# Row sums of attention weights: pairs of key chunks added by accumulating DMA, with bias rows and the adjacency's cast moved to DMA

## The chip, the cores and the metric

One core of one Trainium2 chip. The time is device microseconds of one execution; each kernel was run several times and medians are quoted. Engine names in the profile: PE is TensorE's matmuls, PEld its weight loads, DVE is VectorE, ACT is ScalarE, POOL is GpSimd, SP is SyncE.

## The reference, cut to what matters

Two attention layers over 32 graphs of 512 nodes and 256 channels, 8 heads. Layer 0 has an MLP; layer 1 has none. The mask of layer 0 is the adjacency or its transpose or the diagonal; that of layer 1 is the adjacency.

```python
scores = jnp.einsum('bhqd,bhkd->bhqk', q * scale, k)
scores = jnp.where(allowed[:, None], scores, -jnp.inf)
attn = jax.nn.softmax(scores, axis=-1)
ctx = jnp.einsum('bhqk,bhkd->bhqd', attn, v)
# ... Wo, bias, residual, layernorm, MLP, residual, layernorm; a second layer alike, without the MLP
```

All biases in the inputs are zero, so a wrong or missing bias would not be seen in the result.

## The kernel before

The work runs in 64 slots, one per graph and layer. In a slot the weights are made in eight steps, one for each of two head groups times four chunks of 128 keys: scores on PE, exp on ACT, mask product on DVE, then two products on PE. One gives the context (psA), the other the row sums by a block of ones (psR).

```python
            def scores(self, layer, k):          # PE, then exp on ACT; one PSUM buffer for s
                ...
                nc.scalar.activation(p, s, AF.Exp, scale=SCALE)     # p: 128 x 2048 f32, bufs=4
            def masked(self, layer, k):          # DVE
                nc.vector.tensor_tensor(p, p, m[:, k % NQ, None, :].to_broadcast([P, HPC, N]), ALU.mult)
            def product(self, layer, k):         # PE
                for j in range(HPC): nc.tensor.matmul(a[...], self.v[...], p[:, j, :], ...)
                for j in range(HPC): nc.tensor.matmul(s[...], ones, p[:, j, :], ...)
                if kc < NQ - 1: return
                # copy of a (ACT); transpose of s, reciprocal, transpose, product with cT (DVE)
```

Between these steps PE gets other work. A **forward** slot carries the output projection and the MLP of the graph that was last in layer 0; an **output** slot finishes the graph that was last in layer 1 and makes the masks, the queries, keys and values of the next one. Masks are made by PE transposes of the adjacency in bf16, and DVE empties both PSUM tiles. The adjacency is loaded as int32 and clamped to bf16 on POOL; bias rows are added to residuals on POOL.

## Time and profile before

| | before |
|---|---|
| time | 3852 us |
| PE busy | 3609 us, 94% |
| forward slot, mean | 70.3 us |
| output slot, mean | 48.7 us |
| mean granted clock | 0.992 |

The slot lengths come from the PE timeline of the profiled execution: from the first scores of one slot to the first scores of the next. Unless two slots are named, they are means over 32 forward and 31 output slots (the last output slot runs into the end of the program). Forward slots are all 70.3 us here; the output slots after the first are 48.3 to 49.3 us. Together these 63 make 3758 us; the rest is the start and the last slot. The prediction shows the lines of four slots. In a line of a group the first number after the bar is the busy time and the second the mean length of one instruction; a figure in square brackets at the end of a timeline line is how long the engine stood idle before it and which engine's work ended that.

### The profile page before, as it was taken

The page shows a single profiled execution, that of the slowest core. Times are in us where ns is not written, and L with a number is a line of the kernel's source. Part 1 is how long each engine was busy: PE and PEld are TensorE (multiplying, and loading weights), DVE is VectorE, ACT ScalarE, POOL GpSimd, SP SyncE. Part 2 cuts the span into 40 slices and gives each one's busy share as a digit, 9 for nine tenths or more (in the row PEclk, how much of TensorE's full clock was granted, in tenths as well). Part 3 has the DMA queues.
Part 4 walks back from the last instruction along what each step waited for, and adds up shares of the span by engine and source line. Part 5 has one row for each costly group of instructions (what it writes and reads, how often), then busy time and mean ns, then how long its engine had stood idle before and what let it go on. Part 6 is the DMA issues. An engine that isn't in the chain of part 4 may idle for free.

```text
span 3851.9 us, 51652 instructions
## 1 busy us (share of the span) xinstructions
PE 3608.8 (94%) x21514; PEld 1885.4 (49%) x21514; DVE 2502.6 (65%) x3461; ACT 1603.0 (42%) x1729; POOL 1376.5 (36%) x1545
## 2 busy tenths in 40 slices
PE   6999999999999999999999999998999999999998
PEld 3544536455364554635546355453554535545354
DVE  3666675766757667576665756667576675666766
ACT  3434444434444344343443444434444344343443
POOL 1333333433334243342433424333242333424332
PEclk9999999999999999999999999999999999999999
DMA  2000000000000000000000000000000100000000
GB/s 86 17 23 13 27 12 17 23 23 17 12 17 23 22 23 6 17 28 17 23 6 17 28 17 23 6 22 23 17 23 6 33 12 17 23 6 34 12 1 12
DMA packets 57553, 75.61 MB, mean 20 GB/s; under 512 B 4448, under 2 KB 40416, under 8 KB 57312
## 3 DMA queue, kind: packets, MB, share of 16 engines
q1 hardware_dynamic: 51776, 67.90, 5.2%
q10 hardware_dynamic: 5536, 4.33, 0.4%
q8 instruction: 170, 2.79, 0.3%
q14 instruction: 71, 0.58, 0.0%
HBM read 55.45 MB, written 16.78 MB: 19 GB/s over the span
## 4 chain that ended last, share of the span: by engine, by line
PE 69%; DVE 23%; POOL 5%; ACT 2%; issue 1%; DMA 0%; ACTq 0%; DVEq 0%; POOLq 0%
PE psQK L260 12%; PE psF L391 12%; PE psH L373 12%; DVE p L282 9%; PE psS L273 8%; PE psA L295 7%; PE psV L245 6%; PE psR L303 6%; PE psO L352 5%; POOL rs L330 4%; DVE st L328 3%; DVE x L411 2%; DVE m L214 2%; ACT p L277 2%; DVE y L341 2%; PE psT L233 1%
## 5 line engine op out<-in xcount | busy, mean ns | idle before, releaser
L277 ACT ACTIVATE p<-psS 128x2048 f32<-128x2048 f32 x512 | 961.9, 1879 | 1167.1 <-PE psS L273 1167.1
L282 DVE TENSOR_TENSOR p<-p,m 128x2048 f32<-128x2048 f32 x512 | 1197.4, 2344 | 273.4 <-ACT p L277 273.4
L330 POOL TENSOR_SCALAR rs<-mv 128x1 f32<-128x1 f32 x512 | 499.2, 975 | 1115.0 <-DVE mv L329 1100.3
L295 PE MATMUL psA<-p,v 128*32 128x512 f32 x4096 | 555.8, 615 | 53.6 <-DVE p L282 53.6
L273 PE MATMUL psS<-qT,kT 32*128 32x512 f32 x4096 | 583.9, 640 | 7.1 <-ACT p L277 2.0
L303 PE MATMUL psR<-p,ones 128*32 128x512 f32 x4096 | 544.6, 604 | 0.0
L314 DVE STREAM_TRANSPOSE sT<-psR 128x512 f32<-128x512 f32 x128 | 91.3, 713 | 643.8 <-PE psR L303 643.8
L391 PE MATMUL psF<-w_L_gnn_W,hT 128*128 128x256 f32 x2048 | 459.1, 382 | 0.0
L373 PE MATMUL psH<-xT,w_L_gnn_W 128*128 128x256 f32 x2048 | 459.1, 382 | 0.0
L391 PEld LDWEIGHTS psF<-w_L_gnn_W,hT 128*128 128x128 f32 x2048 | 383.8, 190 | 100.7 <-ACT cT L311 26.8
L373 PEld LDWEIGHTS psH<-xT,w_L_gnn_W 128*128 128x128 f32 x2048 | 383.8, 190 | 98.2 <-ACT xT L236 24.3
L317 POOL TENSOR_TENSOR total<-total,sT 128x16 f32<-128x16 f32 x128 | 29.0, 227 | 985.6 <-DVE sT L314 985.6
L331 POOL TENSOR_TENSOR rs<-rs,neg_half 128x1 f32<-128x1 f32 x512 | 327.1, 639 | 42.7
L273 PEld LDWEIGHTS psS<-qT,kT 32*128 32x128 f32 x4096 | 159.9, 182 | 332.4 <-issue 187.0
L303 PEld LDWEIGHTS psR<-p,ones 128*32 128x32 f32 x4096 | 135.3, 112 | 314.7 <-issue 305.4
L381 ACT ACTIVATE hT<-psH,c_L_gnn_b 128x256 f32<-128x256 f32 x512 | 215.1, 471 | 171.3 <-PE psH L373 169.2
L260 PE MATMUL psQK<-xT,w_L_gnn_Wqkv 128*128 128x512 f32 x512 | 245.0, 611 | 0.0
L252 ACT COPY v<-psV 128x512 f32<-128x512 f32 x128 | 75.0, 586 | 403.3 <-PE psV L245 403.3
L352 PE MATMUL psO<-w_L_gnn_Wo,cT 128*128 128x256 f32 x1024 | 238.4, 386 | 0.5 <-DVE held L768 0.5
L352 PEld LDWEIGHTS psO<-w_L_gnn_Wo,cT 128*128 128x128 f32 x1024 | 189.2, 190 | 72.3 <-ACT kT L263 47.8
L341 DVE TENSOR_TENSOR y<-psO,x 128x256 f32<-128x256 f32 x256 | 104.1, 407 | 152.5 <-PE psO L352 152.5
L295 PEld LDWEIGHTS psA<-p,v 128*32 128x32 f32 x4096 | 80.9, 108 | 230.1 <-issue 101.9
(64 smaller groups left out, 3476.9 us busy)
## 6 DMA issues: line engine op xcount, KB each, us to landing
adj<-in_adj_dram SPq DMA_DIRECT2D x32, 1024.0 KB, 6.2
x<-in_x_dram SPq DMA_DIRECT2D x32, 512.0 KB, 3.9
out_dram<-x SPq DMA_DIRECT2D x32, 512.0 KB, 2.9
w_L_gnn_W<-in_L_gnn_W_dram ACTq DMA_DIRECT2D x2, 1024.0 KB, 10.8
w_L_gnn_Wqkv<-in_L_gnn_Wqkv_dram SPq DMA_DIRECT2D x1, 768.0 KB, 5.0
w_L_gnn_Wo<-in_L_gnn_Wo_dram ACTq DMA_DIRECT2D x2, 256.0 KB, 5.5
s_L_gnn_bo<-in_L_gnn_bo_dram ACTq DMA_DIRECT2D x2, 128.0 KB, 5.7
s_L_gnn_ln_g<-in_L_gnn_ln_g_dram ACTq DMA_DIRECT2D x2, 128.0 KB, 8.4
```

Of the source, the lines that this page charges most:

```text
L245: nc.tensor.matmul(ps[:, j, :], self.xT[:, i, at], proj[layer][0][2][:, i, :], start=(i == 0), stop=(i == ND - 1),)
L260: nc.tensor.matmul(ps, w[:, i, c * P : (c + 1) * P], self.xT[:, i, :], start=(i == 0), stop=(i == ND - 1))
L273: nc.tensor.matmul(s[:, j, :], self.kT[at, hg, kc * P : (kc + 1) * P], self.qT[at, hg, :], start=True, stop=True)
L277: nc.scalar.activation(p, s, AF.Exp, scale=SCALE)
L282: nc.vector.tensor_tensor(p, p, m[:, k % NQ, None, :].to_broadcast([P, HPC, N]), ALU.mult)
L295: nc.tensor.matmul(a[j * HD : (j + 1) * HD, :], self.v[:, kc, h * HD : (h + 1) * HD], p[:, j, :], start=(kc == 0), stop=(kc == NQ - 1),)
L303: nc.tensor.matmul(s[j * HD : (j + 1) * HD, :], ones, p[:, j, :], start=(kc == 0), stop=(kc == NQ - 1))
L330: nc.gpsimd.tensor_scalar(rs, mv[:, 1:2], EPS, None, ALU.add)
L331: nc.gpsimd.tensor_tensor(rs, rs, neg_half[:, 0:1], ALU.pow)
L352: nc.tensor.matmul(ps[:, j, :], self.cT[:, k, at], wo[layer][:, k, :], start=(k == 0), stop=(k == ND - 1))
L373: nc.tensor.matmul(ps[:, j, :], w1[:, c, at], self.xT[:, c, h * 2 * P : (h + 1) * 2 * P], start=(c == 0), stop=(c == ND - 1),)
L391: nc.tensor.matmul(ps, self.hT[h][:, f, j * P : (j + 1) * P], w2[:, f, :], start=(f == 0), stop=(f == NF - 1))
```

## The change

It takes three of the eight row sums of a slot off PE: an accumulating DMA adds the weights of chunk k+1 to those of chunk k, and PE sums the result once. Only the last pair (6, 7) is left to PE. The accumulating DMAs are issued from POOL, and POOL is relieved of other work: bias rows are added by accumulating DMA too (so x1, onto which one is added, is loaded as well), and the load casts the adjacency. DVE makes two codes from it, edge and none (1 where there is no edge). The mask of layer 1 comes from none and is emptied by ACT in place of DVE. The operations at the ends of slots are put in another order, and some buffers are cut to make room for six p.

```diff
-            nc.gpsimd.tensor_tensor(dst, src, row[:, None, :].to_broadcast([P, NQ, D]), ALU.add)
+            nc.gpsimd.dma_start(out=dst, in_=row[:, None, :].to_broadcast([P, NQ, D]), accum_op=ALU.add)
...
-                nc.vector.tensor_scalar(self.m1[:, i, :], ps, 0.0, None, ALU.not_equal)
+                nc.scalar.activation(self.m1[:, i, :], ps, AF.Copy, bias=1.0, scale=-1.0)
...
-                p = work.tile([P, HPC, N], F32, tag="p", name=f"p_{self.b}_{k}", bufs=4)
+                p = work.tile([P, HPC, N], F32, tag="p", name=f"p_{self.b}_{k}", bufs=6)
...
+            def pair(self, k):
+                nc.gpsimd.dma_start(out=self.p[k], in_=self.p[k + 1], accum_op=ALU.add)
+            def sums(self, k, first=False, last=False):      # the matmuls with ones; if last, DVE's chain
... forward slot:
+            g.pair(0)            # step 3
+            g.pair(2)            # step 5, then g.sums(0, first=True)
+            g.sums(2, last=True) # step 6
+            g.pair(4)            # after product 5; then sums 6, 7 and 4 at the end
... output slot:
+            g.pair(0)            # step 2
                 new.residual()   # step 3: two bias rows, now DMAs
+            g.pair(2)            # step 4
+            g.sums(0, first=True)  # step 5
+            g.sums(2, last=True)   # step 6
+            g.pair(4)            # step 7; then sums 6, 7 and 4
```

More of the change, by code (lines that the diff above doesn't have):

```diff
@@ L166, in value_bias, with add_row @@
                 nc.vector.tensor_tensor(bov[layer], ps, bo[layer], ALU.add)
-        def add_row(dst, src, row):
-            nc.gpsimd.tensor_tensor(dst, src, row[:, None, :].to_broadcast([P, NQ, D]), ALU.add)
+        def add_row(dst, row):
+            nc.gpsimd.dma_start(out=dst, in_=row[:, None, :].to_broadcast([P, NQ, D]), accum_op=ALU.add)
         class Graph:
@@ L183, in load @@
             def load(self):
-                nc.sync.dma_start(
-                    out=self.tile("x", [NQ, D]), in_=x[self.b].rearrange("(c p) d -> p c d", p=P)
-                )
-                nc.sync.dma_start(
-                    out=self.tile("adj", [NQ, N], I32, bufs=1), in_=adj[self.b].rearrange("(c p) k -> p c k", p=P)
+                rows = x[self.b].rearrange("(c p) d -> p c d", p=P)
+                nc.sync.dma_start(out=self.tile("x", [NQ, D]), in_=rows)
+                nc.sync.dma_start(out=self.tile("x1", [NQ, D]), in_=rows)
+                nc.gpsimd.dma_start(
+                    out=self.tile("adj", [NQ, N], BF16, bufs=1), in_=adj[self.b].rearrange("(c p) k -> p c k", p=P)
                 )
             def code(self):
-                code = self.tile("edge", [NQ, N], BF16, bufs=1)
-                for i in range(NQ):
-                    nc.gpsimd.tensor_scalar(code[:, i, :], self.adj[:, i, :], 1.0, -0.25, ALU.min, ALU.max)
+                nc.vector.tensor_scalar(self.tile("edge", [NQ, N], BF16, bufs=1), self.adj, 0.0, None, ALU.max)
+                nc.vector.tensor_scalar(self.tile("none", [NQ, N], BF16, bufs=1), self.adj, 0.0, None, ALU.is_equal)
                 self.tile("m0", [NQ, N], BF16)
@@ L199, in residual @@
             def residual(self):
-                add_row(self.tile("x1", [NQ, D]), self.x, bov[0])
-                add_row(self.x, self.x, be2)
+                add_row(self.x1, bov[0])
+                add_row(self.x, be2)
             def mask0(self, i):
@@ L220, in mask1 @@
                     nc.tensor.matmul(
-                        ps[:, k * P : (k + 1) * P], self.edge[:, k, here], ident_b, start=True, stop=True
+                        ps[:, k * P : (k + 1) * P], self.none[:, k, here], ident_b, start=True, stop=True
                     )
-                nc.vector.tensor_scalar(self.m1[:, i, :], ps, 0.0, None, ALU.not_equal)
+                nc.scalar.activation(self.m1[:, i, :], ps, AF.Copy, bias=1.0, scale=-1.0)
             def transpose(self, src, h):
                 if h == 0:
-                    self.tile("xT", [ND, N])
+                    self.tile("xT", [ND, N], bufs=1)
                 ps = ps_d.tile([P, ND, 2 * P], F32, tag="d", name=f"psT_{self.b}_{h}")
@@ L282, in masked, with product @@
                 nc.vector.tensor_tensor(p, p, m[:, k % NQ, None, :].to_broadcast([P, HPC, N]), ALU.mult)
-            def product(self, layer, k):
+            def product(self, k):
                 hg, kc = divmod(k, NQ)
-                p = self.p.pop(k)
                 if kc == 0:
-                    self.acc[hg] = (
-                        ps_a.tile([P, N], F32, tag="acc", name=f"psA_{self.b}_{hg}"),
-                        ps_a.tile([P, N], F32, tag="sum", name=f"psR_{self.b}_{hg}"),
-                    )
-                a, s = self.acc[hg]
+                    self.acc[hg] = ps_a.tile([P, N], F32, tag="acc", name=f"psA_{self.b}_{hg}")
                 for j in range(HPC):
@@ L295, in product @@
                     nc.tensor.matmul(
-                        a[j * HD : (j + 1) * HD, :],
+                        self.acc[hg][j * HD : (j + 1) * HD, :],
                         self.v[:, kc, h * HD : (h + 1) * HD],
-                        p[:, j, :],
+                        self.p[k][:, j, :],
                         start=(kc == 0),
@@ L301, in product @@
                     )
+                if kc == NQ - 1:
+                    if hg == 0:
+                        self.tile("cT", [ND, N], bufs=1)
+                    nc.scalar.copy(self.cT[:, hg, :], self.acc[hg])
+            def pair(self, k):
+                nc.gpsimd.dma_start(out=self.p[k], in_=self.p[k + 1], accum_op=ALU.add)
+            def sums(self, k, first=False, last=False):
+                hg = k // NQ
+                if first:
+                    self.total = ps_a.tile([P, N], F32, tag="sum", name=f"psR_{self.b}_{hg}")
                 for j in range(HPC):
                     nc.tensor.matmul(
-                        s[j * HD : (j + 1) * HD, :], ones, p[:, j, :], start=(kc == 0), stop=(kc == NQ - 1)
+                        self.total[j * HD : (j + 1) * HD, :], ones, self.p[k][:, j, :], start=first, stop=last
                     )
-                if kc < NQ - 1:
+                if not last:
                     return
-                if hg == 0:
-                    self.tile("cT", [ND, N], bufs=1)
-                cT = self.cT[:, hg, :]
-                nc.scalar.copy(cT, a)
-                sT = small.tile([P, N // HD, HD], F32, tag="sT", name=f"sT_{self.b}_{hg}", bufs=2)
-                nc.vector.transpose(sT.rearrange("p a b -> p (a b)"), s)
+                sT = small.tile([P, N // HD, HD], F32, tag="sT", name=f"sT_{self.b}_{hg}", bufs=1)
+                nc.vector.transpose(sT.rearrange("p a b -> p (a b)"), self.total)
                 r = small.tile([P, N // HD], F32, tag="r", name=f"r_{self.b}_{hg}")
@@ L318, in product @@
                 nc.gpsimd.tensor_tensor(total, total, r, ALU.add)
-                rT = small.tile([P, N], F32, tag="rT", name=f"rT_{self.b}_{hg}", bufs=2)
+                rT = small.tile([P, N], F32, tag="rT", name=f"rT_{self.b}_{hg}", bufs=1)
                 nc.vector.transpose(rT, r[:, :, None].to_broadcast([P, N // HD, HD]))
-                nc.vector.tensor_tensor(cT, cT, rT, ALU.mult)
+                nc.vector.tensor_tensor(self.cT[:, hg, :], self.cT[:, hg, :], rT, ALU.mult)
             def statistics(self, y, n, i):
@@ L383, in residual1 @@
             def residual1(self):
-                add_row(self.x1, self.x1, b2)
+                add_row(self.x1, b2)
                 self.tile("x2", [NQ, D])
@@ L397, in norm2 @@
                 y, stats = self.y.pop(i)
-                z = small.tile([P, D], F32, tag="z", name=f"z_{self.b}_{i}", bufs=3)
+                z = small.tile([P, D], F32, tag="z", name=f"z_{self.b}_{i}", bufs=2)
                 self.affine(z, y, stats, g2, self.x[:, i, :], 2, i)
@@ L442, in slot_forward @@
             if layer == 1:
-                add_row(g.x2, g.x2, bov[1])
+                add_row(g.x2, bov[1])
             last.project(0, 0)
@@ L449, in slot_forward @@
             attend(g, layer, 2)
-            g.product(layer, 0)
+            g.product(0)
             last.norm1(0)
@@ L456, in slot_forward @@
             attend(g, layer, 3)
-            g.product(layer, 1)
+            g.product(1)
+            g.pair(0)
             last.norm1(2)
@@ L466, in slot_forward @@
             last.residual1()
-            if later is not None:
-                later.code()
-            g.product(layer, 2)
+            g.product(2)
             attend(g, layer, 5)
+            g.pair(2)
             for f in range(0, NF, 2):
                 last.hidden(1, f)
-            g.product(layer, 3)
+            g.sums(0, first=True)
+            g.product(3)
             last.mlp(0)
@@ L485, in slot_forward @@
             last.norm3(1)
-            g.product(layer, 4)
+            g.sums(2, last=True)
+            g.product(4)
             g.scores(layer, 7)
@@ L493, in slot_forward @@
             g.masked(layer, 7)
-            g.product(layer, 5)
             last.transpose(last.x2, 0)
-            g.product(layer, 6)
+            g.product(5)
+            g.pair(4)
             last.value(1, 0)
+            g.product(6)
             last.transpose(last.x2, 1)
-            g.product(layer, 7)
+            g.sums(6, first=True)
             last.query_key(1, 0, 0)
             last.query_key(1, 1, 0)
+            g.product(7)
+            g.sums(7)
+            g.sums(4, last=True)
             last.value(1, 1)
+            if later is not None:
+                later.code()
         def slot_output(g, layer, last, new, later):
@@ L512, in slot_output @@
             if layer == 1:
-                add_row(g.x2, g.x2, bov[1])
+                add_row(g.x2, bov[1])
             if last:
@@ L527, in slot_output @@
                 new.transpose(new.x, 0)
-            g.product(layer, 0)
+            g.product(0)
+            g.pair(0)
             attend(g, layer, 3)
@@ L537, in slot_output @@
                 new.residual()
-            g.product(layer, 1)
-            for i in range(NQ):
-                attend(g, layer, 4 + i)
-                if new:
-                    new.mask0(i)
-                    new.mask1(i)
-                g.product(layer, 2 + i)
-            if later is not None:
-                later.code()
+            g.product(1)
+            attend(g, layer, 4)
+            if new:
+                new.mask0(0)
+                new.mask1(0)
+            g.product(2)
+            g.pair(2)
+            attend(g, layer, 5)
+            if new:
+                new.mask0(1)
+                new.mask1(1)
+            g.sums(0, first=True)
+            g.product(3)
+            attend(g, layer, 6)
+            if new:
+                new.mask0(2)
+                new.mask1(2)
+            g.product(4)
+            g.sums(2, last=True)
+            attend(g, layer, 7)
+            if new:
+                new.mask0(3)
+                new.mask1(3)
+            g.product(5)
+            g.pair(4)
             g.masked(layer, 7)
@@ L550, in slot_output @@
                 new.value(0, 0)
-            g.product(layer, 6)
+            g.product(6)
+            g.sums(6, first=True)
             if new:
                 new.query_key(0, 0, 0)
-            g.product(layer, 7)
+                new.query_key(0, 1, 0)
+            g.product(7)
+            g.sums(7)
+            g.sums(4, last=True)
             if new:
-                new.query_key(0, 1, 0)
                 new.value(0, 1)
+            if later is not None:
+                later.code()
         with tc.manual_schedule():
```

## The prediction

> **What bounds the kernel now.** I read the page first: busy time, then the costliest groups.
>
> ```profile
> PE 3608.8 (94%) x21514; PEld 1885.4 (49%) x21514; DVE 2502.6 (65%) x3461; ACT 1603.0 (42%) x1729; POOL 1376.5 (36%) x1545
> ...
> L282 DVE TENSOR_TENSOR p<-p,m 128x2048 f32<-128x2048 f32 x512 | 1197.4, 2344 | 273.4 <-ACT p L277 273.4
> ...
> L303 PE MATMUL psR<-p,ones 128*32 128x512 f32 x4096 | 544.6, 604 | 0.0
> ```
>
> TensorE (PE) is busy 94% of 3852 us. The row sums psR are 4096 instructions, 8 for each of 512 key chunks. 94% is an average, so I cut the timeline into its repeating slots (64: one graph and layer each). There are two kinds. A **forward** slot carries the MLP of the previous graph; an **output** slot carries the masks of the next one. The windows over two output slots and then two forward slots:
>
> ```profile
> core 0: us, PE busy (x) PEld busy (x) DVE busy (x) ACT busy (x) POOL busy (x), PEclk, DMA share, GB/s
> 944.50:992.80 48.30, 43.78 (x284) 18.20 (x281) 35.76 (x40) 20.49 (x17) 20.70 (x18) 0.96 0.04 12
> 992.80:1041.13 48.33, 43.24 (x290) 18.13 (x289) 35.40 (x40) 21.08 (x18) 14.78 (x14) 1.00 0.04 12
> 1041.13:1111.45 70.32, 68.56 (x385) 40.45 (x384) 42.74 (x68) 28.99 (x36) 24.45 (x30) 1.00 0.07 23
> 1111.45:1181.77 70.32, 68.57 (x386) 40.46 (x385) 42.73 (x68) 28.99 (x36) 26.79 (x34) 1.00 0.07 23
> ```
>
> The forward slot is PE-bound (68.6 of 70.3). The output slot has 5 us in which PE waits. 32 x (48.3 + 70.3) = 3796, the rest is start and end. The PE timeline around two early score steps of a forward slot shows a second limit:
>
> ```profile
> 1050.55 1.14 PE L273 MATMUL psS<-qT,kT 32*128 32x512 f32 x8
> 1051.62 1.06 PE L295 MATMUL psA<-p,v 128*32 128x512 f32 x8
> 1052.50 1.04 PE L303 MATMUL psR<-p,ones 128*32 128x512 f32 x8
> 1053.69 1.14 PE L273 MATMUL psS<-qT,kT 32*128 32x512 f32 x8
> ```
>
> By the ACT timeline the exponential of the first psS runs 1051.76 to 1053.64 (1.88 us). There is one psS buffer, so the next scores wait for it: **a score step cannot be shorter than 3.14 us** (1053.69 - 1050.55), whatever PE saves inside it. In the output slot the mask steps follow DVE:
>
> ```profile
> 1024.66 1.88 ACT L277 ACTIVATE p<-psS 128x2048 f32<-128x2048 f32 x1 [2.49 <-PE psS L273]
> ```
> ```profile
> 1026.54 0.38 PE L208 MATMUL psM<-edge,ident_b 128*128 128x512 bf16 x1 [1.95 <-DVE m L214]
> ```
> ```profile
> 1008.15 2.16 POOL L330 TENSOR_SCALAR rs<-mv 128x1 f32<-128x1 f32 x1
> 1010.39 0.58 POOL L331 TENSOR_TENSOR rs<-rs,neg_half 128x1 f32<-128x1 f32 x1
> ```
>
> PE waits 1.95 us for a mask buffer that DVE has not emptied, after the exp had long started; and Pool finishes the fourth rs of the slot only at 1010.97, which is 18.2 us into the slot that began at 992.80.
>
> **What the Trainium skill says.** (1) "DMA: Bandwidth & Descriptors", section SWDGE vs HWDGE vs iDMA: accumulating and casting DMAs can be issued from GpSimd alone, and one SWDGE queue is allocated. The trace of before has no such DMA, so neither is shown. Its section Specifications gives about 1 us to the first byte on that path. (2) "Collectives: The Full Stack", section on the bandwidth ceiling: a reducing DMA is not slowed by the add but by two reads per write, about 31 GB/s per engine halved. Not shown in before either: its plain loads run at 67.9 MB / (5.2% x 3852 us) = 339 GB/s. (3) "SBUF — State Buffer", section Who interferes with whom: a DVE instruction with two SBUF inputs contends with a GpSimd instruction that reads SBUF. The trace agrees: rs takes 0.22 us alone and 2.16 us beside the 2.3 us mask product.
>
> **The change, part by part.** I walk both slots; times are from the slot's start.
>
> *Removed on PE.* Three of eight row sums per slot: 192 groups. A sum that no wait follows costs 0.97 us from its start to the next instruction (by the same timeline 1066.70 to 1067.67), so 192 x 0.97 = 186 us if all counted. They do not.
>
> *Forward slot.* The sums leave steps 2, 3 and 4; the later steps get a sum back for each they lose (0 at step 5, 2 at step 6; 6, 7 and 4 at the end). Step 2 is already 3.14 us: nothing saved. Step 3 was 3.51 and falls to 3.14: 0.4. Step 4 holds 7 us of hidden layer: 0.9 saved. At the end a 1.6 us wait for p goes behind the value product, but that now waits some 1.3 us for its transposed input behind an exp: 0.3. Sum 1.6 us; 32 x 1.6 = **50 us saved**, if the third DMA lands: it is issued after the fourth rs3 (about 58.3) and wanted by sum 4 at about 66, so it has 7.6 us.
>
> *Cost of one accumulate.* 1.05 MB at 16 x 31 / 2 = 248 GB/s is 4.2 us of all engines (estimate from Collectives; doubling the trace's plain 3.1 us gives 6.2). Before it 1.0 us for the descriptors; after it a tail of 1.35 us (the 512 KB store lands in 2.9 us, of which 1.55 is data at 339 GB/s). Issue to landing: 6.5 us. A bias row (512 KB) holds the engines for half as long, 2.1 us.
>
> *Output slot, gains.* Removing Pool's adds (2.4 and 4.5 us, beside which DVE ops took 2.46 for 0.41 and 3.24 for 2.28) and moving m1 to ACT (4 x 0.6) takes some 5.4 us off DVE. With no late DMA I walk PE to 45.7 instead of 48.3.
>
> *Output slot, the new wait.* Pair 0 stands on Pool behind the fourth rs: issued at 18.2, landed at 24.7. PE wants sum 0 at 22.3: **2.4 us late**. Pool then issues the two bias rows, and only then pair 2. On one queue: engines start at 19.2, then 4.2 + 2.1 + 2.1 + 4.2 = 31.8, landed at 33.1. PE, after sum 0 at 25.7, product, scores, masks and product, wants sum 2 at 29.3: **3.8 us late**. DVE's sum chain stands in program order ahead of mask product 6 and of the mask that frees the value's PSUM buffer. So the wait passes through: sums end 34.1, DVE chain 36.7, mask product 39.0, mask 39.6, value 41.6, then product, sum, query/key, product, two sums, value: 51.8. Pair 4 is issued near 36 and lands near 42.5, wanted at 49: in time. The slot is 51.8 - 48.3 = 3.5 longer; 32 x 3.5 = **110 us lost**.
>
> *Start.* The second graph's code now stands on DVE and waits for its cast load before the first mask product: about 4 us, once. ACT gains 128 copies of 0.59 us (75 us) at 42% busy, DVE 64 short operations at slot ends: hidden.
>
> Sum: 3852 - 50 + 110 + 4 = 3916.
>
> **The rivals.** *(a) The accumulate is as fast as a copy* (3.1 us of engines): pair 0 lands at 23.7, pair 2 at 29.9, the output slot is 48.6, about even; 3852 - 50 + 9 + 4 = 3815. For it: the add is free by the skill. Against: two reads. If in addition the landing took under 4 us, the output slot would be 45.7 and the kernel 3720; the store's 2.9 us for half the bytes speaks against that. *(b) Engines at twice the plain time* (6.2 us): pair 2 lands at 39, output slot 57.9, forward slot saves only 0.6: about 4140. Smaller packets or slow descriptor generation (512 rows of 1 KB in each bias row) would look the same. *(c) PE work alone decides* and the DMAs are hidden: 3852 - 186 = 3666. For it: PE is 94% busy. Against: the 3.14 us score step and 18.2 us at which Pool becomes free. *(d) DVE slows down under Pool's descriptor writing*: a few us, since DVE has slack in forward slots.
>
> **Range and chances.** The walk gives 3916, rival (a) 3815, rival (b) 4140. The one number that the profile cannot give is the accumulate's rate. Somebody chose three pairs out of four, which looks like tuning by measurement, so I lean a little to the fast side: 3900. Range 3745 to 4110, wide towards slow since each us of engine time costs the output slot about three. Faster than 3775 needs an accumulate at least as quick as a copy with a short landing: 0.21. Within 2% (3775 to 3929): 0.42. Slower: 0.37.
>
> **What would show it.** Right: psR with 2560 instructions in place of 4096; in output slots PE waits for DMA at psR for p_0 and more for p_2; forward slots near 68.7 us with no DMA wait; output slots near 52; score steps 2 and 3 of the forward slot at 3.14. An accumulate's issue to landing near 6.5 us, pair 2 longer through the queue. Wrong: landings under 4.5 us (then rival a or c), landings over 9 us with waits in forward slots at sum 4 too (b), or a slot that starts pair 0 well before 18 us.

## The result, and the profile after

| | before | after |
|---|---|---|
| time, median | 3851.9 us | 4204.4 us |
| PE busy | 3609 us | 3599 us |
| forward slot, mean | 70.3 us | 71.8 us |
| output slot, mean | 48.7 us | 57.7 us |
| mean granted clock | 0.992 | 0.952 |

The ratio is 1.091 (95% interval 1.089 to 1.093). The time lies above the whole stated range.

The page of the changed kernel, with busy times, the group that sums rows, and the DMA issues from POOL (count, size, median us from issue to landing):

```profile
PE 3598.5 (86%) x19978; PEld 1839.2 (44%) x19978; DVE 2318.3 (55%) x3397; ACT 1664.3 (40%) x1857; POOL 1248.4 (30%) x1641
...
L311 PE MATMUL psR<-p,ones 128*32 128x512 f32 x2560 | 380.8, 687 | 297.1 <-DMA p<-p 297.0
...
p<-p POOLq DMA_DIRECT2D x192, 1024.0 KB, 8.1
...
x<-bov POOLq DMA_DIRECT2D x64, 512.0 KB, 9.0
...
x<-s_L_gnn_ln_b POOLq DMA_DIRECT2D x32, 512.0 KB, 13.8
x<-s_L_gnn_b POOLq DMA_DIRECT2D x32, 512.0 KB, 5.5
```

PE lost 1536 instructions of psR and 164 us of its busy time, and 297 us of waiting for the pairs' DMA stand in front of what is left. The total busy time of PE fell by only 10 us, although fewer instructions run. The windows over two output and two forward slots that follow each other tell where:

```profile
core 0: us, PE busy (x) PEld busy (x) DVE busy (x) ACT busy (x) POOL busy (x), PEclk, DMA share, GB/s
1017.54:1076.39 58.85, 44.09 (x265) 17.43 (x264) 31.36 (x38) 23.09 (x22) 15.44 (x19) 0.91 0.56 99
1076.39:1135.18 58.79, 45.17 (x265) 17.61 (x265) 31.40 (x39) 23.10 (x22) 13.21 (x17) 0.91 0.43 81
1135.18:1206.25 71.07, 66.88 (x361) 39.46 (x360) 41.03 (x69) 28.86 (x36) 23.83 (x33) 1.00 0.32 67
1206.25:1277.33 71.08, 66.89 (x362) 39.47 (x361) 41.01 (x68) 28.85 (x36) 25.71 (x34) 1.00 0.42 82
```

These two output slots are among the longest (the others after the first last 57.0 to 59.1 us), and these two forward slots among the shortest. Over all slots the output slot grew by 9.1 us and the forward slot by 1.5: 32 x 10.6 = 339 us of the 341 between the two profiled spans (3851.9 and 4193.2). The granted clock in the two output slots is 0.91. The timeline of PE in the second output slot shows both waits and the slow instructions behind them:

```profile
1102.72 1.93 PE L311 MATMUL psR<-p,ones 128*32 128x512 f32 x8 [3.94 <-DMA p<-p]
1104.43 1.94 PE L289 MATMUL psA<-p,v 128*32 128x512 f32 x8
1106.29 2.09 PE L272 MATMUL psS<-qT,kT 32*128 32x512 f32 x8
...
1115.45 1.88 PE L311 MATMUL psR<-p,ones 128*32 128x512 f32 x8 [5.05 <-DMA p<-p]
1117.26 1.97 PE L272 MATMUL psS<-qT,kT 32*128 32x512 f32 x8
```

PE waits 3.94 us for pair 0, and from 26.3 us in the slot the three groups of the same kinds that took 1.04, 1.06 and 1.14 us before take about 2. It then waits 5.05 us for pair 2, which it can use at 39.06 us. The timeline of POOL in the same slot, and SP's single DMA in it:

```profile
1094.56 0.91 POOL L303 DMA_DIRECT2D p<-p  x1
1095.57 1.30 POOL L169 DMA_DIRECT2D x<-bov  x1
1096.34 1.83 POOL L169 DMA_DIRECT2D x<-s_L_gnn_ln_b  x1
1097.79 1.28 POOL L303 DMA_DIRECT2D p<-p  x1
```
```profile
1095.08 0.38 SPq L418 DMA_DIRECT2D out_dram<-x  x1
```

All four accumulates of the slot's middle (two pairs, two bias rows) are issued within 4.5 us, and a 512 KB store joins them. The window over the wait says how fast they drain:

```profile
1102.00:1115.00 13.00, 7.67 (x42) 1.90 (x42) 1.54 (x2) 2.95 (x3) 0.00 (x0) 0.74 1.05 191
```

The DMA engines are busy throughout (the share is of packet times, which can overlap, so 1.05 is possible) and write 191 GB/s, so 1.05 MB takes 5.5 us of them. That is the rate of a mixture: 191 GB/s x 13 us is 2.5 MB, the size of the two rows, pair 2 and most of the store.

In these two forward slots no DMA is waited for (over all 32, PE has five such waits, 3.4 us in all). What ends the slot late is at its tail. DVE's timeline there:

```profile
1188.86 0.71 DVE L318 STREAM_TRANSPOSE sT<-psR 128x512 f32<-128x512 f32 x1
1189.61 0.25 DVE L320 RECIPROCAL r<-sT 128x16 f32<-128x16 f32 x1
1189.89 0.71 DVE L324 STREAM_TRANSPOSE rT<-r 128x512 f32<-128x512 f32 x1
1190.71 0.69 DVE L325 TENSOR_TENSOR cT<-cT,rT 128x512 f32<-128x512 f32 x1
...
1192.99 2.27 DVE L281 TENSOR_TENSOR p<-p,m 128x2048 f32<-128x2048 f32 x1
```

And PE's, with the wait for that mask product:

```profile
1195.31 1.06 PE L289 MATMUL psA<-p,v 128*32 128x512 f32 x8 [2.05 <-DVE p L281]
```

The chain for the first head group's sums (2.5 us) now stands in DVE's busiest stretch, ahead of mask product 6. Before, it followed chunk 3's sums in step 5, when DVE had been idle for 12 us. The wait of 2.05 us stands in every forward slot. In 15 of the 32 PE is slow after it and the slot takes over 72 us, as here:

```profile
873.90:946.47 72.57, 68.37 (x361) 39.78 (x361) 41.04 (x69) 28.86 (x36) 23.83 (x33) 0.98 0.31 66
934.04 1.39 PE L289 MATMUL psA<-p,v 128*32 128x512 f32 x8 [2.06 <-DVE p L281]
936.41 1.87 PE L311 MATMUL psR<-p,ones 128*32 128x512 f32 x8
```

### The profile page after: what moved, and what is told of

Same layout as the page of the kernel before. It is cut to its first block, busy times and chain, and to the rows that moved or that the text cites. A ratio compares the mean times of both kernels' runs of the same rounds, so it can differ in the third digit from the quotient of the medians.

```text
span 4193.2 us, 49139 instructions
## 1 busy us (share of the span) xinstructions
PE 3598.5 (86%) x19978; PEld 1839.2 (44%) x19978; DVE 2318.3 (55%) x3397; ACT 1664.3 (40%) x1857; POOL 1248.4 (30%) x1641
## 4 chain that ended last, share of the span: by engine, by line
PE 60%; DVE 15%; DMA 15%; POOL 5%; ACT 3%; issue 2%; DVEq 0%; POOLq 0%; ACTq 0%
DMA p<-p 14%; PE psF L395 11%; PE psH L377 11%; PE psQK L259 11%; PE psS L272 8%; PE psR L311 6%; DVE p L281 5%; PE psA L289 4%; PE psV L244 4%; PE psO L356 4%; POOL rs L334 4%; ACT p L276 3%; DVE st L332 2%; DVE y L345 1%; DVE rT L324 1%
## 5 line engine op out<-in xcount | busy, mean ns | idle before, releaser
L281 DVE TENSOR_TENSOR p<-p,m 128x2048 f32<-128x2048 f32 x512 | 1163.3, 2278 | 110.9 <-ACT p L276 110.9
L272 PE MATMUL psS<-qT,kT 32*128 32x512 f32 x4096 | 630.6, 687 | 68.6 <-ACT p L276 68.6
L289 PE MATMUL psA<-p,v 128*32 128x512 f32 x4096 | 577.1, 637 | 68.8 <-DVE p L281 68.8
L311 PE MATMUL psR<-p,ones 128*32 128x512 f32 x2560 | 380.8, 687 | 297.1 <-DMA p<-p 297.0
L272 PEld LDWEIGHTS psS<-qT,kT 32*128 32x128 f32 x4096 | 170.6, 195 | 441.8 <-issue 249.7
L345 DVE TENSOR_TENSOR y<-psF,x 128x256 f32<-128x256 f32 x128 | 54.4, 425 | 545.6 <-PE psF L395 545.6
L311 PEld LDWEIGHTS psR<-p,ones 128*32 128x32 f32 x2560 | 68.9, 115 | 459.2 <-DMA p<-p 342.4
L289 PEld LDWEIGHTS psA<-p,v 128*32 128x32 f32 x4096 | 94.9, 112 | 305.4 <-issue 160.1
```

The lines of the kernel that those rows point to most:

```text
L272: nc.tensor.matmul(s[:, j, :], self.kT[at, hg, kc * P : (kc + 1) * P], self.qT[at, hg, :], start=True, stop=True)
L289: nc.tensor.matmul(self.acc[hg][j * HD : (j + 1) * HD, :], self.v[:, kc, h * HD : (h + 1) * HD], self.p[k][:, j, :], start=(kc == 0), stop ...
L311: nc.tensor.matmul(self.total[j * HD : (j + 1) * HD, :], ones, self.p[k][:, j, :], start=first, stop=last)
```

## The experiments

**Theory after the result.** (1) In the output slot the pairs come late, because the queue drains at 5.5 us per 1.05 MB and pair 2 queues behind pair 0, two bias rows and a store; PE then runs slowly after each wait. (2) In the forward slot the moved DVE chain takes back what the pairs save. **Rivals**: the other parts of the change (masks on ACT, bias rows by DMA, DVE's code at the slot end) lengthen the slots; the slow PE after the waits is the cause and not a symptom; the way through POOL is what is slow, not the accumulate.

### Pairs in forward slots only, and no pairs at all

```diff
 # shortened; output slot only (first run); both kinds of slot (second run)
-            g.pair(0); g.pair(2); g.pair(4); the sums at their later places
+            g.sums(k, first=k % 4 == 0, last=k % 4 == 3)    # after each g.product(k)
```

> The changed kernel, but with the accumulating DMAs of pairs in forward slots only; output slots sum each key chunk on PE, as the kernel before did. Theory (the output slot is longer because PE waits for late accumulates and then runs slowly for a while): output slot falls from 58.8 to 46 to 48 us, forward slot stays at 71, total about 3820. Rival (the other parts of the change, m1 on ACT, the code on DVE, bias rows by DMA, lengthen the output slot): it stays over 50 us, total over 3910.

> The changed kernel without any accumulated pair: every chunk has its own row sum on PE; bias rows by DMA, cast by the load, m1 on ACT and the new order at the slot ends stay. Theory: the output slot is as in the run with forward pairs only (46 to 48 us), the forward slot about 70, because its three saved sums are hidden by the score step of 3.14 us and eaten by a wait at its end: total about 3790, within 1% of the run with forward pairs only. Rival (pairs do save PE time in forward slots): this run is over 1.5% slower than the run with forward pairs only.

Measured: 3766.3 us with forward pairs only (ratio 0.978, 0.976 to 0.980) and 3701.9 us with no pairs (0.961, 0.960 to 0.963). The windows of the run without pairs, a forward and an output slot:

```profile
1069.29:1139.19 69.90, 69.08 (x385) 40.40 (x384) 41.06 (x68) 28.95 (x36) 23.11 (x31) 1.00 0.22 38
1139.19:1183.31 44.12, 42.84 (x290) 17.91 (x289) 31.26 (x38) 22.91 (x22) 12.76 (x16) 1.00 0.39 60
```

The output slot fell from 57.7 to 44.1 us in both runs, lower than expected. So the pairs alone make the output slot long, and the other parts of the change together are a gain of 4.6 us against before (48.7). My expectation for the two totals was too high by 54 and 88 us, mainly since I had put the output slot at 46 to 48. The second result went against the expectation that the two runs are within 1%: forward pairs, as the change has them, cost 64 us (forward slots of 71.9 us with them and 69.9 without), and the rival, that they save, fell too.

### Bias rows at the end of the output slot

```diff
-                new.residual()          # step 3
...
+            if new:
+                new.residual()          # after value(0, 1), the last work of the slot
```

> The changed kernel, with the two bias rows of the output slot issued at its end in place of between pair 0 and pair 2. Theory (pair 2 is late because it queues behind two bias rows): it lands some 6 to 7 us sooner, the output slot falls from 58.8 to about 52.5, total about 4000. Rival (pair 2 is late by its own transfer or by descriptor generation): total stays over 4130.

Measured: 4032.7 us (1.047, 1.045 to 1.049); the output slot is 52.3 us, expected 52.5. PE's timeline at sum 2, in a slot that begins at 1035.00:

```profile
1068.28 1.06 PE L311 MATMUL psR<-p,ones 128*32 128x512 f32 x8 [0.19 <-DMA p<-p]
```

Sum 2 starts at 33.3 us of the slot in place of 39.1: pair 2 landed 5.8 us sooner. By this, an estimate, the two bias rows take the engines some 2.9 us each. The rest of the queue is still there, and sum 0 still waits 3.7 us.

### PE kept at work while it waits

```diff
+                for n in range(warm):       # 4 ahead of sum 0, 5 ahead of sum 2; zeros is 128 x 32
+                    for j in range(HPC):
+                        nc.tensor.matmul(self.total[j * HD : (j + 1) * HD, :], zeros,
+                                         self.p[(3, 4)[k // 2]][:, j, :], start=first and n == 0, stop=False)
```

> The changed kernel, with products of zero weights (4 groups ahead of sum 0, 5 ahead of sum 2) that keep PE at work while it waits in output slots; they add zero, so the result stays right. Theory (PE runs at half its rate for some us after a long wait, because its clock is lowered): the 8 psR instructions after the wait take 1.05 in place of 1.9 us, as do the psA and psS after them, mean granted clock back to 0.98 or more, output slot 54 to 55.5 us, total about 4080. Rival (PE is slowed by the DMA's own traffic in SBUF, or by anything that lasts as long as the DMA): psR stays at 1.9 us and the total at 4190 or more.

Measured: 4195.4 us (1.089, 1.087 to 1.091), the same as the changed kernel. PE's timeline at both sums, slot from 1075.49:

```profile
1101.92 1.07 PE L323 MATMUL psR<-p,ones 128*32 128x512 f32 x8 [0.48 <-DMA p<-p]
...
1114.50 1.06 PE L323 MATMUL psR<-p,ones 128*32 128x512 f32 x8 [3.47 <-DMA p<-p]
1115.50 1.60 PE L274 MATMUL psS<-qT,kT 32*128 32x512 f32 x8
```

Sum 0 takes 1.07 us in place of 1.93, so idling is what slows PE, as "TensorE: Matmul & The Clock Gate", Part 1, says of the clock after an idle window of about 3.4 us. It is neither SBUF traffic nor the DMA: the queue drains beside sum 0 here as before. At sum 2 some 3 us of wait were left after the products of zeros, and sum 2 took 1.06 us in some slots and over 1.8 in others. Yet the time did not move. Sum 0 starts at 26.4 us of the slot and sum 2 at 39.0, as in the changed kernel (26.3 and 39.1): both are set by the landing, and slow PE work between them was hidden in the second wait. Over all slots the output slot became 0.3 us shorter (57.4 in place of 57.7) and the forward slot 0.3 longer (72.1 in place of 71.8), since PE was slow after the wait of 2.05 us in 22 forward slots in place of 15. I had expected 54 to 55.5 us for the output slot; the half of my theory that put the slow work on the path fell.

### The DVE chain moved out of the way in forward slots

```diff
-            g.sums(2, last=True)        # step 6, ahead of product 4
...
             last.norm3(3)
+            g.pair(4)
+            g.sums(2, last=True)
             g.masked(layer, 7)
```

> The changed kernel; in forward slots sum 2 with DVE's chain for it (two transposes, reciprocal, product) and pair 4 move behind norm3 of the last row block, so that mask product 6 no longer stands behind the chain. Theory (the forward slot gained nothing because the chain, moved from DVE's idle time into its busy time, delays mask product 6 by some 2.5 us and PE waits 2.05 us for it): that wait goes, forward slot 71.07 to about 68.8 us, total about 4130; output slots unchanged at 58.8. Rival (the forward slot waits for a late pair or for PE's clock): forward slot stays near 71, total over 4180.

Measured: 4109.9 us (1.067, 1.065 to 1.069). The forward slot is 69.0 us on average and the output slot 57.9, as it was. Two neighbours:

```profile
1054.02:1112.75 58.73, 43.78 (x265) 17.41 (x264) 31.38 (x39) 23.09 (x22) 13.18 (x17) 0.91 0.43 81
1112.75:1181.50 68.75, 66.87 (x361) 39.37 (x360) 40.98 (x69) 28.85 (x36) 23.84 (x33) 1.00 0.33 69
```

The chain is the whole loss of the forward slot: without it in front of mask product 6, the wait of 2.05 us shrinks to 0.38, no slot takes over 72 us, and the slot is nearly as long as the prediction's walk made it (70.3 - 1.6 = 68.7). Pair 4 moved too, but its wait had been 3.4 us in the whole run, too little for the 94 us gained.

### An accumulate and a copy, each alone on the queue

No pairs in the sums; in each forward slot one accumulate and one plain copy of 1 MB from p into scratch tiles, issued from POOL when its queue is empty. To make room, p has four buffers again.

```diff
+                if k == 0:
+                    nc.gpsimd.dma_start(out=accum, in_=self.p[k + 1], accum_op=ALU.add)
+                elif k == 2:
+                    nc.gpsimd.dma_start(out=copied, in_=self.p[k + 1])
```

> No pairs in the sums. In forward slots GpSimd issues one 1 MB accumulate from p into a scratch tile (after chunk 1's sum) and one plain copy of the same size into another (after chunk 3's sum), at times when its queue is otherwise empty. Theory (the accumulate needs two reads for each write): it lands in 7 to 8 us, the plain copy in 4.5 to 5.5 us. Rival (the way through GpSimd, descriptors or landing, is what is slow): both land within 1 us of each other, near 7.5 us. Time near that of the run without pairs, 3700.

Measured (one run, profiled; its time, 3703.6 us, is not used), by the DMA issues:

```profile
accum<-p POOLq DMA_DIRECT2D x32, 1024.0 KB, 7.0
copied<-p POOLq DMA_DIRECT2D x32, 1024.0 KB, 4.7
```

And the windows over one accumulate and over one copy (DMA share and GB/s at the end):

```profile
1093.00:1099.00 6.00, 6.00 (x33) 4.98 (x35) 5.45 (x5) 3.33 (x9) 0.92 (x2) 1.00 0.84 171
1112.40:1117.50 5.10, 5.10 (x27) 3.62 (x26) 3.85 (x6) 1.88 (x1) 2.58 (x2) 1.00 0.53 206
```

The way through POOL is not slow in itself: the copy lands in 4.7 us, where the fit in "DMA: Bandwidth & Descriptors", Anatomy of one DMA, gives 2.0 + 1.05 MB / 436 GB/s = 4.4 as an estimate. The accumulate lands 2.3 us later. Its packets hold the engines for about 5.1 us (0.84 x 6.00, of which the window has 1.03 of 1.05 MB), those of the copy for 2.7 (0.53 x 5.10), 1.9 times as long. That agrees with two reads per write, though no run shows the reads themselves.

### The better versions

Forward pairs with the moved chain, output slots without pairs; then the same with pair 4 in the output slot too.

> Pairs in forward slots only, with the chain moved as in the run that moves it; output slots sum every chunk on PE. Theory: output slot 44.1, forward slot 68.8, total 32 x 112.9 + 48 = about 3660, faster than the run without pairs (3702). Rival (pairs cost the forward slot something besides the chain): at or above 3702.

> As the run with forward pairs and the moved chain, and pair 4 accumulated in output slots as well (pairs 0 and 2 there stay on PE). Theory (pair 4 has over 10 us in the output slot, so it is not waited for): output slot about 43.2, total about 3632. Rival (a pair in the output slot always ends in a wait, for its landing or for the score step): at or above 3660.

Measured: 3667.6 us (0.952, 0.950 to 0.954) and 3699.6 us (0.960, 0.959 to 0.962). The windows of the first, output and forward:

```profile
1176.05:1220.16 44.11, 42.83 (x289) 17.89 (x288) 31.28 (x39) 22.91 (x22) 10.55 (x14) 1.00 0.21 37
1220.16:1288.90 68.74, 66.86 (x361) 39.43 (x360) 40.97 (x69) 28.83 (x36) 23.82 (x33) 1.00 0.33 69
```

This is the best kernel. Forward pairs save 34 us of the 3701.9 once the chain is out of the way. Pair 4 in the output slot lands in time, sums 7 and 4 run without a gap, and still the slot is 45.0 us in place of 44.1. The total is not the 3632 us that I expected but above the rival's 3660. PE's timeline there:

```profile
1168.12 0.38 PE L207 MATMUL psM<-edge,ident_b 128*128 128x512 bf16 x1 [1.26 <-DVE m L213]
...
1170.92 1.99 PE L244 MATMUL psV<-w_L_gnn_Wqkv,xT 128*128 128x256 f32 x8 [0.93 <-DVE m L213]
```

The two sums, of chunks 4 and 5, that leave the steps of the masks uncover waits for DVE's mask copies (1.26 and 0.93 us; without the pair 0.65 and none), and the sum that comes back stands at the end of the slot, where it counts in full. My expectation of 43.2 us missed that.

### What the rest of the change is worth

Both from the run without pairs. First the bias rows back on POOL, then the layer-1 mask back on DVE.

```diff
-            nc.gpsimd.dma_start(out=dst, in_=row[:, None, :].to_broadcast([P, NQ, D]), accum_op=ALU.add)
+            nc.gpsimd.tensor_tensor(dst, dst, row[:, None, :].to_broadcast([P, NQ, D]), ALU.add)
```
```diff
-                nc.scalar.activation(self.m1[:, i, :], ps, AF.Copy, bias=1.0, scale=-1.0)
+                nc.vector.tensor_scalar(self.m1[:, i, :], ps, 0.0, None, ALU.is_equal)
```

> The run without pairs, with the bias rows added by GpSimd again as in the kernel before (everything else of that run stays). Theory (the gain of the run without pairs comes mostly from GpSimd's adds no longer blocking DVE's two-input operations in the output slot): output slot 45.5 to 47 us in place of 44.1, total 3745 to 3795. Rival (the adds did not matter, as DVE has slack): total within 15 us of 3702.

> The run without pairs, with the layer-1 mask emptied from PSUM by DVE again, as in the kernel before. Theory (DVE's 4 x 0.6 us per output slot were on PE's path through the mask buffers): output slot about 45.5 to 46.5, total 3745 to 3780. Rival (the adds' removal alone has freed DVE enough): total within 15 us of 3702.

Measured: 3871.6 us (1.005, 1.003 to 1.007) and 3738.3 us (0.971, 0.969 to 0.972). The bias rows by DMA are worth 170 us, far more than the 43 to 93 expected; the mask on ACT 36 us, just under what was expected. The output slot with the adds on POOL is 49.6 us. POOL's two adds, DVE's work beside them, and PE's wait:

```profile
1204.85 2.36 POOL L169 TENSOR_TENSOR x<-x,bov 128x1024 f32<-128x1024 f32 x1
1207.16 2.40 POOL L169 TENSOR_TENSOR x<-x,s_L_gnn_ln_b 128x1024 f32<-128x1024 f32 x1
```
```profile
1204.91 2.45 DVE L415 TENSOR_SCALAR x<-y,mv,rs 128x256 f32<-128x256 f32 x1 [0.46 <-POOL rs L335]
1207.28 4.43 DVE L281 TENSOR_TENSOR p<-p,m 128x2048 f32<-128x2048 f32 x1
```
```profile
1212.36 0.58 PE L207 MATMUL psM<-edge,ident_b 128*128 128x512 bf16 x1 [3.70 <-DVE m L213]
```

DVE takes 2.45 us for what takes 0.41 alone and 4.43 for 2.28. For the mask product, with its two inputs in SBUF, that is the contention of the prediction's third citation. Together it costs 4.2 us in DVE's busiest stretch; PE then waits up to 3.7 us for a mask buffer (0.65 without the adds) and runs slowly after it. With the adds alone put back, the kernel is slower than before, although the mask stays on ACT: what is left of the change (the order, DVE's codes, the buffers) is no gain in that company. No run parts it further.

## Why the prediction was wrong

The direction was the walk's (3916, 1.7% slower), but the kernel is 9.1% slower, and the stated number was 3900, with more chance given to no clear change (0.42) than to slower (0.37). Against 3916, 288 us are missing: the output slot grew by 9.1 us and not 3.5 (some 180 us), the forward slot by 1.5 us in place of shrinking by 1.6 (some 100). By its steps:

- **The slots of before.** The first window of the prediction starts 1.04 us late (that slot's first scores stand at 943.46), so the slot took 49.3 us, not 48.3; the mean is 48.7. This is small beside what follows.
- **Sums removed, score step.** Right: 2560 psR instructions, steps 2 and 3 of the forward slot at 3.14 us (the PE timeline has psS at 1144.60, 1147.74 and 1150.88).
- **Forward slot, 1.6 us saved.** Wrong by 3.1 us, some 100 us in all (71.8 in place of 68.7). The walk took DVE's times from before and forgot that the change moves the sum chain from step 5 into the tail, where PE waits 2.05 us for mask product 6 and in 15 of 32 slots runs slowly for a while, which makes the slot 1.4 us longer still. With the chain moved away the slot is 69.0 us, nearly as walked, and the kernel 94 us faster.
- **Pair 0 issued at 18.2 us.** Right: 1094.56 - 1076.39 = 18.2. PE could start sum 0 at 26.3, predicted 24.7.
- **Pair 2 landed at 33.1 us.** Wrong: sum 2 starts at 39.1 in the slot shown (38.5 in the median slot), and this is the mis-sized sum that failed most. The cost of one accumulate was put at 4.2 us of all engines; alone it took 5.1, and the mixed queue drains at 5.5 per 1.05 MB. A bias row was put at 2.1; the run with the rows last gives 2.9. The store, 1.6 us by the plain rate, was left out. As an estimate, 2 x (0.9 to 1.3) + 2 x 0.8 + 1.6 = 5.0 to 5.8 us of the 6.0; only the rows' part was tested by taking them away. At the median that is 5.4 us a slot, some 170 us.
- **18.7 us from the start of sum 2 to the slot's end.** Took 19.7 in the slot shown (39.1 to 58.8). The walk did not have PE's slow stretch after the wait; with PE kept at work the same stretch took 18.9 (39.0 to 57.9).
- **Rivals.** (b), engines at twice the plain time, was nearest: 4140. An accumulate does hold the engines about twice as long as a copy (5.1 and 2.7 us); its 6.2 us came from doubling 3.1, the rate of the loads. The lean to the fast side, for the sake of the look of tuning, had no measurement under it and went the wrong way. The range should have reached past the worst case of a queue, since, by the prediction's own sum, every us of engine time per MB is paid about three times in one slot.
- **Relief of DVE.** DVE's busy time in an output slot fell by 4.0 us (35.4 to 31.4), since the two new codes (1.4 us) run there too; 5.4 had been walked. Yet the slot that the walk gave without late DMAs, 45.7, was still too long: with all sums left on PE it is 44.1. This error made the walk's total higher and so hid a part of the others, by luck. Late DMA ate a gain larger than the one the pairs were meant to bring.

What stays open: why PE is slow after the wait of 2.05 us in some forward slots and not in others, and what the order at the slot ends and the buffers are worth alone.

## What to carry to other kernels

An engine that is 94% busy over a whole run can still be bound elsewhere in the steps from which work is removed: walk the steps, with the shortest repeat that a single buffer allows, before a removal is counted. For work handed to a DMA, add up everything on the queue between issue and need, stores from other queues included, and take the rate of that kind of transfer from a short measurement. When operations change places in program order, redo the timeline of every engine that runs them: here a chain of 2.5 us that had been free cost 2 us per slot and slowed PE in some. And take a slot's length over many slots: two neighbours had shown 71.1 us where the mean was 71.8.

## What the Trainium skill lacked or had wrong

- "DMA: Bandwidth & Descriptors": no figure for an accumulate within SBUF. Measured here from POOL: 1 MB lands in 7.0 us alone against 4.7 for a copy, and holds the engines for about 5.1 us against 2.7.
- "Collectives: The Full Stack", section on the bandwidth ceiling: two reads per write fit the direction, but its 31 GB/s per engine, halved and times 16, is 248 GB/s, an estimate that carries a figure for rings over to SBUF; here an accumulate alone writes 171 / 0.84 = 204 GB/s of busy engines, and the mixed queue 191.
- No page says what a broadcast row costs as the source of an accumulate: 512 KB in rows of 1 KB took 5.5 us from issue to landing alone on the queue (x<-s_L_gnn_b in the run without pairs), and about 2.9 us of the engines in the output slot's queue.
- "TensorE: Matmul & The Clock Gate", Part 1, speaks of idle windows of about 3.4 us. In the changed kernel a wait of 2.05 us was followed by slow PE (psR at 1.87 us in place of 1.06) in forward slots of over 72 us, 15 of 32, and not in those under 71.3, 13 of 32; the page has no figure for so short a wait.
